# Spectra by array halves in layer 0, and other step weights, in a four-layer image network

## The chip, the cores and the metric

The kernel runs on one core of one Trainium2 chip. The metric is the device time of one execution in microseconds (us). Times of single instructions, waits and stages come from one profiled execution.

The engines that matter: TensorE (PE; its weight loads stand apart as PEld), VectorE (DVE), ScalarE (ACT), GpSimd (POOL), and SyncE (SP), which only issues transfers. Each works through its own instructions in order, and the engines wait for each other by semaphores. Matmuls write to PSUM, which is eight banks of 128 x 512 floats.

## The reference

The input is four images of 48 channels, 256 x 256, in float32. Four layers follow, each as `x = x + L(gn(x))`, where `gn` is a group norm over three channels and the whole image.

```python
# layer 0: 1x1 conv to 288 channels, 3x3 depthwise conv, then per 8x8 patch
q, k, v = split(dwconv(conv1x1(x)), 3)                 # 96 channels each
out = irfft2(rfft2(q_patch) * rfft2(k_patch))          # 8x8 patches
out = conv1x1(v * layernorm_over_channels(out))
# layer 1: 1x1 conv, filter in the patches' spectrum, 3x3 depthwise, gelu gate, 1x1 conv
# layer 2: box means, the box of each pixel from a small conv net:
out = (A + D - B - C) / area                           # 4 bilinear samples of the 2-d running sum
# layer 3: 1x1 conv, 3x3 depthwise, gelu gate, 1x1 conv, filter in the patches' spectrum
```

A patch's spectrum is computed as a product with a small matrix of cosines and sines. Of an 8 x 8 real patch it has 64 real numbers: 34 cosine sums ("every": four frequencies that are their own mirror, and 30 pairs) and 30 sine sums ("pairs").

## The kernel before

**Two streams.** `run` (L1210) lets two generators take turns. Stream "a" does layers 0 and 1 of image 0, then of images 1, 2 and 3, then layer 3 of all four. Stream "b" does the first statistics of the images and some weights, then layer 2 of images 0 to 3. Layer 2 of an image starts when its layer 1 is done, so it is issued beside layers 0 and 1 of the next image; layer 2 of image 3 stands beside layer 3 of images 0 to 2, and layer 3 of image 3 must wait for it. Each `yield` gives a weight; the stream with the smaller sum of weights goes next (`advance`, L1228), and a stream that must wait for the other takes over its sum. The weights thus settle how the two streams' instructions are mixed in every engine's order. A scheduler may still move instructions within that order, except the ones passed through `pinned`. Stream "a" issues its transfers on SP's queue, stream "b" on GpSimd's; each stream has its own PSUM banks, five for "a" and two (with a third for weights) for "b". A bank is handed out anew when its last reader is done.

**Layer 0** (L392) goes by units of four blocks of 128 pixels, 128 units an image, as a pipeline. In step n: `convolve` of unit n (24 full records and 8 tail records on TensorE into four banks, L353 and L361; four copies to `qkv` by ScalarE, L434); `inverse` of unit n-2; `spectra` of n-1; `turn` of n-5 (four transposes, L493, and a copy, L495); `project` of n-6 for every other strip (L505, L507); `gate` of n-4. A block has 128 pixels, that is two patches, one on partitions 0 to 63 and one on 64 to 127. `spectra` treats both at once: the 128 spectral numbers of the two patches are 68 cosine rows and 60 sine rows, so a matmul with 128 x 128 matrices gives q (L438), k (L439) and k with cosine and sine exchanged (L440), 384 columns each. ScalarE copies q (L442), VectorE makes the two products t1 and t2 (L445, L446), and `inverse` adds two matmuls (L454, L455) in one bank. VectorE takes the statistics of the result (L457), and ScalarE copies it to `o` (L458).

`convolve2` (L346) treats the ninth tap's rest, 58 rows, in `tails`: its two row halves of the array, partitions 0 to 57 and 64 to 121, hold two different pixel rows.

**Layer 1** (L585) has three stages: A, 1x1 conv, stored to DRAM (L623); B, filter and depthwise conv by channel group (L654, L667, L668); C, turn and project (L741, L754).

**Layer 2** (L838) first makes the running sums (`sums`, L774), then works through 32 pieces, two to a strip of eight rows (both image halves). A piece has four steps. In each, GpSimd issues 16 gathers into one of three buffers `V` (L974), and VectorE weights and adds the buffer of the step before (`add`, L981: L985, four times L987, L988). Convolution (L876, L885), projection (L901) and boxes for later pieces are mixed in. When both pieces of a strip are done, `finish` (L992) loads the strip of x, turns the result on TensorE (L999), adds it (L1006), and stores the strip. It is called in the three steps after the strip's last: the load stands in the first of these, the store in the last, both on GpSimd's queue between gathers.

**Layer 3** (L1066) is a pipeline of 128 units an image, two yields each.

Of the kernel before, what the change touches and what calls it, by code (L numbers as in the profile page):

```python
# [8 lines left out]
F32 = mybir.dt.float32  # L9
# [10 lines left out]
NS = 16  # L20
CP = 2 * C
PW = 258
# [36 lines left out]
def constants():  # L59
    own, pairs = _frequencies()  # L60
    every = own + pairs
# [5 lines left out]
    f1, f2, a1, a2 = (np.zeros((128, 128)) for _ in range(4))  # L67
    for k in range(2):
        px = slice(64 * k, 64 * k + 64)
        for i, f in enumerate(every):  # L70
            r, w = 34 * k + i, (1 if f in own else 2) / 64
            f1[px, r] = cos[f]
            a1[r, px] = w * cos[f]
            if f in pairs:
                f2[px, r] = -sin[f]
                a2[r, px] = -w * sin[f]
        for i, f in enumerate(pairs):
            r, w = 68 + 30 * k + i, 2 / 64
            f1[px, r] = -sin[f]
            f2[px, r] = cos[f]  # L80
            a1[r, px] = -w * cos[f]
            a2[r, px] = -w * sin[f]
# [69 lines left out]
    for a in range(2):  # L152
# [9 lines left out]
        "c_dft": np.stack([f1, f2, a1, a2, rf, rf.T], 1),  # L162
# [13 lines left out]
class Net:  # L176
    def __init__(self, ctx, tc, a, out):
# [13 lines left out]
        dft = self.load("c_dft", [128, 6, 128])  # L191
        self.f1, self.f2, self.a1, self.a2, self.rf, self.ri = (dft[:, i, :] for i in range(6))
# [199 lines left out]
    def layer0(self, x, mr, y):  # L392
        nc, a = self.nc, self.a
        st = self.stat.tile([CP, 129, 6], F32, name=self.nm("st"), tag="st" + self.stream, bufs=1)
        with ExitStack() as ctx:
# [40 lines left out]
            def spectra(t):  # L436
                q1, k1, k2 = self.bank(), self.bank(), self.bank()
                nc.tensor.matmul(v3(q1), self.f1, t.qkv[:, :, 0:96], start=True, stop=True)  # L438
# [3 lines left out]
                nc.scalar.copy(qs[:], q1[:, 0:384])  # L442
                t.t1 = sb.tile([128, 384], F32, name="t1", tag="t1")
                t.t2 = sb.tile([128, 384], F32, name="t2", tag="t2")
                nc.vector.tensor_mul(t.t1[:], qs[:], k1[:, 0:384])  # L445
                nc.vector.tensor_mul(t.t2[:], qs[:], k2[:, 0:384])  # L446

            def inverse(t):
# [5 lines left out]
                nc.tensor.matmul(po[:, 0:384], self.a1, t.t1[:], start=True, stop=False)  # L454
                nc.tensor.matmul(po[:, 0:384], self.a2, t.t2[:], start=False, stop=True)  # L455
# [382 lines left out]
    def layer2(self, x, mr, y, table):  # L838
# [3 lines left out]
        with ExitStack() as ctx:  # L842
# [148 lines left out]

            def finish(t, j):  # L992

                if j == 0:
                    t.xt = sb.tile([CP, 8, PW], F32, name="xt", tag="xt", bufs=1)
                    self.load_rows(t.xt, x, 8 * t.s, 8)
# [8 lines left out]
                v = t.xt[:, 2 * j : 2 * j + 2, 1:257]  # L1005
# [3 lines left out]
                if j == 3:  # L1009
                    self.store_rows(y, t.xt, 8 * t.s, 8)  # L1010
# [10 lines left out]
            for n in range(2):  # L1021
                for h in range(2):
                    convolve(pieces[n], h)
                    look(pieces[n + 1], h)
                    for j in range(2):
                        project(pieces[n], 2 * h + j)
                if n == 0:
                    boxes(pieces[0])
                yield 30
            last, done = None, None  # L1030
            for n in range(len(pieces) + 1):
                t = piece(n)
                for h in range(4):
# [10 lines left out]
                    yield 11  # L1044
# [17 lines left out]
                    yield 11  # L1062
# [3 lines left out]
    def layer3(self, x, mr, y):  # L1066
        nc, a = self.nc, self.a
        with ExitStack() as ctx:
# [97 lines left out]
            for n in range(len(units) + 7):  # L1166
# [5 lines left out]
                yield 4  # L1172
# [10 lines left out]
                yield 4  # L1183
# [120 lines left out]
```

## Time and profile before

| | us |
|---|---|
| runs, median of 3 | 20775.92 (20766.17 to 20789.14) |
| profiled execution | 20767.55 |
| its span on the core | 20765.8 |
| TensorE busy | 18830.0 (91%) |
| VectorE busy | 10830.0 (52%) |
| GpSimd busy | 8656.1 (42%) |
| ScalarE busy | 5784.0 (28%) |

By the first and last instructions of their lines, the stages of the profiled execution are: layer 0 of image 0 from 145 to 1967 us and its layer 1 from 1975 to 3536, both without gathers; then three times about 4165 us for layers 0 and 1 of images 1 to 3 beside layer 2 of the image before (layer 0 of image 1 from 3606 to 5651, its layer 1 from 5679 to 7699); then layer 3 of images 0 to 2 beside layer 2 of image 3, from about 16040 to 19733; then layer 3 of image 3 alone, to the end. Layer 1's stages took 352, 905 and 276 us in image 0 and 535, 1145 and 280 us in image 1. The gathers run from 3996 to 7395, 8155 to 11564, 12324 to 15723 and 16546 to 19709 us.

The page's 40 slices are 519 us each. A digit is the busy share in tenths; PEclk is the granted clock of TensorE in the same way. In the tables of groups a line gives instructions, busy time, mean length, and the idle time of the engine just before them with what ended it.

### The profile page before, as it was taken

To read this page: it belongs to the slowest core of one execution; us is meant where nothing else is said; L and a number is where in the kernel's file an instruction comes from. 1 tells how busy PE (TensorE), PEld (TensorE's weight loads), DVE (VectorE), ACT (ScalarE), POOL (GpSimd) and SP (SyncE) were. 2 spreads that over 40 slices of the span, in tenths; PEclk is the share of its full clock that TensorE was granted. 3 is DMA by queue.
4 is the path that set the end of the run, shared out by engine and by line. 5 is a ranking of instruction groups with operands and counts; after the bars stand their busy time and mean duration, and the time that the engine had idled before them with its cause. 6 is when DMAs were issued, how large, how long until landed. Compare 5 with 4: busy or idle time off the path is not lost.

```text
span 20769.8 us, 232624 instructions
## 1 busy us (share of the span) xinstructions
PE 18834.6 (91%) x79032; PEld 11959.3 (58%) x79032; DVE 10828.5 (52%) x21947; ACT 5789.6 (28%) x12185; POOL 8657.6 (42%) x8899
## 2 busy tenths in 40 slices
PE   7998798999878889998788899997888999999999
PEld 4566335666543346665433466654334787878888
DVE  4544322477764544777645437776554255555511
ACT  2333212333331123333311233333112211111111
POOL 1000000177754511777545216775552066666600
PEclk9899799999968999999689999996889999999999
DMA  4623876555588975555889755558898566767633
GB/s 113 134 57 80 232 215 201 133 129 131 128 244 223 239 214 133 129 132 126 239 229 233 222 131 126 130 127 232 232 234 225 142 150 150 158 149 158 147 76 74
DMA packets 2494455, 3403.86 MB, mean 164 GB/s; under 512 B 595078, under 2 KB 2069630, under 8 KB 2382731
## 3 DMA queue, kind: packets, MB, share of 16 engines
q1 hardware_dynamic: 1906184, 2081.72, 38.6%
q0 software_dynamic: 452944, 1110.52, 21.7%
q10 hardware_dynamic: 134144, 196.73, 4.2%
q8 instruction: 635, 10.40, 0.2%
q14 instruction: 548, 4.49, 0.1%
HBM read 2450.46 MB, written 802.77 MB: 157 GB/s over the span
## 4 chain that ended last, share of the span: by engine, by line
PE 73%; DMA 14%; DVE 5%; POOL 3%; issue 2%; SPq 1%; ACT 1%; ACTq 0%; DVEq 0%; POOLq 0%
PE ps L353 23%; PE ps L361 5%; PE ps L876 5%; PE ps L654 4%; PE ps L668 3%; PE ps L667 3%; DMA ct<-cD 3%; PE ps L623 3%; PE ps L754 3%; POOL V L974 3%; PE ps L1120 2%; PE ps L901 2%; PE ps L505 2%; PE ps L811 2%; PE ps L741 1%
## 5 line engine op out<-in xcount | busy, mean ns | idle before, releaser
L974 POOL DMA_INDIRECT V<-t,idx x8192 | 8242.8, 1006 | 4831.8 <-issue 2343.8
L353 PE MATMUL ps<-W,A 128*128 128x288 f32 (+1 forms) x24576 | 5571.9, 375 | 96.1 <-DMA A<-x 26.9
L353 PEld LDWEIGHTS ps<-W,A 128*128 128x128 f32 x24576 | 4298.4, 192 | 1246.5 <-issue 530.0
L214 POOL DMA_DIRECT2D X<-x x192 | 144.0, 755 | 4247.4 <-DMA x<-xt 3037.6
L987 DVE TENSOR_TENSOR V<-V 128x1536 f32<-128x1536 f32 (+3 forms) x2048 | 1843.6, 901 | 19.5
L985 DVE TENSOR_TENSOR V<-V,w 128x3072 f32<-128x3072 f32 x512 | 1713.4, 3346 | 28.4 <-DMA V<-t,idx 18.0
L654 PE MATMUL ps<-hg,ct 128*128 128x512 f32 x2304 | 1268.7, 678 | 404.0 <-DMA ct<-cD 322.8
L623 PE MATMUL ps<-win,xp 48*128 48x288 f32 x4096 | 1097.0, 626 | 512.0 <-DVE xp L610 231.2
L434 ACT COPY qkv<-ps 128x288 f32<-128x288 f32 x2048 | 764.4, 401 | 2680.0 <-PE ps L353 1197.9
L876 PE MATMUL ps<-A,W 128*96 128x512 f32 x3072 | 1490.3, 621 | 3.0 <-issue 3.0
L668 PE MATMUL ps<-yh,ht 65*128 65x512 f32 x2304 | 1187.1, 661 | 141.4 <-DMA yh<-ys 123.7
L361 PE MATMUL ps<-W,B 58*128 58x288 f32 (+1 forms) x8192 | 1267.9, 392 | 29.5 <-DMA B<-x 16.7
L1100 DVE TENSOR_TENSOR gp<-gl,ps 128x192 f32<-128x192 f32 x1024 | 354.3, 352 | 1710.2 <-ACT gl L1099 1709.4
L457 DVE BATCH_NORM_STATS2 bs<-ps 128x6 f32<-128x96 f32 x2048 | 389.7, 252 | 1638.1 <-PE ps L455 1637.9
L667 PE MATMUL ps<-ys,tt 128*128 128x512 f32 x2304 | 1177.7, 633 | 66.3 <-DVE ys L658 33.1
L623 PEld LDWEIGHTS ps<-win,xp 48*128 48x128 f32 x4096 | 692.9, 276 | 884.9 <-ACT hs L630 286.4
L654 PEld LDWEIGHTS ps<-hg,ct 128*128 128x128 f32 x2304 | 472.5, 212 | 1047.2 <-issue 940.4
L1099 ACT ACTIVATE gl<-ps 128x192 f32<-128x192 f32 x1024 | 332.1, 331 | 2614.0 <-PE ps L353 2359.1
L672 DVE TENSOR_TENSOR gt<-gl,ps 128x512 f32<-128x512 f32 x576 | 395.5, 688 | 1248.1 <-PE ps L668 1247.6
L361 PEld LDWEIGHTS ps<-W,B 58*128 58x128 f32 x8192 | 762.5, 187 | 450.8 <-issue 343.1
L876 PEld LDWEIGHTS ps<-A,W 128*96 128x96 f32 x3072 | 488.8, 169 | 859.0 <-issue 846.0
L658 DVE COPY ys<-ps 128x512 f32<-128x512 f32 x576 | 397.1, 690 | 1087.2 <-PE ps L654 885.7
(182 smaller groups left out, 24313.1 us busy)
## 6 DMA issues: line engine op xcount, KB each, us to landing
hD<-hs SPq DMA_DIRECT2D x64, 4608.0 KB
hg<-hD SPq DMA_DIRECT2D x288, 1024.0 KB
gD<-gt SPq DMA_DIRECT2D x144, 1024.0 KB
gs<-gD SPq DMA_DIRECT2D x64, 2304.0 KB
V<-t,idx POOLq DMA_INDIRECT x8192
A<-x SPq DMA_DIRECT2D x512, 193.5 KB
xt<-x SPq DMA_DIRECT2D x256, 387.0 KB
A<-x ACTq DMA_DIRECT2D x512, 193.5 KB
```

Of the source, the lines that this page charges most:

```text
L353: nc.tensor.matmul(to(q, b), A[:, r + q, 128 * b + g : 128 * b + g + 128], W[:, g, :], start=b == 0 and g == 0, stop=b == 1 and g == 2,)
L361: nc.tensor.matmul(to(q, b), B[p, r // 2, 128 * b : 128 * b + 128], W[p, 3, :], start=b == 1, stop=b == 0)
L434: nc.scalar.copy(t.qkv[:, 2 * q + b, :], banks[2 * b + q][:, 0:288])
L623: nc.tensor.matmul(ps[:, :288], xp[64 * h : 64 * h + 48, b, :], win[64 * h : 64 * h + 48], start=True, stop=True,)
L654: nc.tensor.matmul(ps[:].rearrange("p (s n) -> p s n", n=32), ct[:, c, :], hg[:, :, c, :], start=True, stop=True)
L667: nc.tensor.matmul(order(ps[:]), to[:, q, :], pick(yo, 128, q), start=True, stop=False)
L668: nc.tensor.matmul(order(ps[:]), ho[:, q, :], pick(yho, NZ, q), start=False, stop=True)
L754: nc.tensor.matmul(pp[:CP, :], pr[:, q, :], got[q][:], start=q == 0, stop=q == 2)
L876: m = nc.tensor.matmul(to[q], W[:, g, :], A[:, q:4:2, g : g + 256], start=q == 0 and g == 0, stop=q == 1 and g == 2,)
L974: nc.gpsimd.indirect_dma_start(out=V[:, k, 4 * cr : 4 * cr + 4, :].rearrange("p e c -> p (e c)"), out_offset=None, in_=table, in_offset=ba ...
L985: self.pinned(nc.vector.tensor_mul(Vm, Vm, wm.unsqueeze(2).to_broadcast([128, 64, 48])))
L987: nc.vector.tensor_add(V[:, :, 0:n, :], V[:, :, 0:n, :], V[:, :, n : 2 * n, :])
```

## The change

1. **Layer 0's spectra.** The matrices are now for one patch: 64 x 64 `f1` and `f2`, and `back` with `a1` above `a2`. `fq` holds `[f1 f1]` and `fk` holds `[f1 f2]` for each half of the partitions, so that one matmul with 64 rows gives 128 outputs for one patch. `spectra` makes four such matmuls instead of three full ones, q and k for each half, into four banks; ScalarE copies q twice, and VectorE makes two products, one for each half. `inverse` makes two matmuls with all 128 rows and 64 outputs, one into the lower and one into the upper half of the bank's partitions.
2. **Layer 2's strips.** `finish` neither loads nor stores. `fetch` loads a strip (the first before the loop), and the store and the next load are issued in the second and the fourth step of the piece after the one in which the strip is finished; the last store follows the loop. There is still one buffer.
3. **Step weights.** The two yields of a gather step go from 11 to 12, those of layer 3 from 4 to 4.4.

```diff
@@ layer0
             def spectra(t):
-                q1, k1, k2 = self.bank(), self.bank(), self.bank()
-                nc.tensor.matmul(v3(q1), self.f1, t.qkv[:, :, 0:96], start=True, stop=True)
-                nc.tensor.matmul(v3(k1), self.f1, t.qkv[:, :, 96:192], start=True, stop=True)
-                nc.tensor.matmul(v3(k2), self.f2, t.qkv[:, :, 96:192], start=True, stop=True)
-                qs = sb.tile([128, 384], F32, name="qs", tag="qs")
-                nc.scalar.copy(qs[:], q1[:, 0:384])
-                t.t1 = sb.tile([128, 384], F32, name="t1", tag="t1")
-                t.t2 = sb.tile([128, 384], F32, name="t2", tag="t2")
-                nc.vector.tensor_mul(t.t1[:], qs[:], k1[:, 0:384])
-                nc.vector.tensor_mul(t.t2[:], qs[:], k2[:, 0:384])
+                q, k = [self.bank() for _ in range(2)], [self.bank() for _ in range(2)]
+                half = lambda p: slice(64 * p, 64 * p + 64)
+                for to, f, c in ((q, self.fq, 0), (k, self.fk, 96)):
+                    for p in range(2):
+                        nc.tensor.matmul(
+                            v3(to[p]), f[half(p), :], t.qkv[half(p), :, c : c + 96], start=True, stop=True
+                        )
+                t.product = []
+                for p in range(2):
+                    qs = sb.tile([128, 384], F32, name="qs", tag=f"qs{p}")
+                    nc.scalar.copy(qs[:], q[p][:, 0:384])
+                    t.product.append(sb.tile([128, 384], F32, name="tp", tag=f"tp{p}"))
+                    nc.vector.tensor_mul(t.product[p][:], qs[:], k[p][:, 0:384])
...
                 po = self.bank()
-                nc.tensor.matmul(po[:, 0:384], self.a1, t.t1[:], start=True, stop=False)
-                nc.tensor.matmul(po[:, 0:384], self.a2, t.t2[:], start=False, stop=True)
+                for p in range(2):
+                    nc.tensor.matmul(
+                        po[64 * p : 64 * p + 64, 0:384], self.back, t.product[p][:], start=True, stop=True
+                    )
@@ layer2
+            strip = {}
+
+            def fetch(s):
+                if s < NS:
+                    strip[s] = sb.tile([CP, 8, PW], F32, name="xt", tag="xt", bufs=1)
+                    self.load_rows(strip[s], x, 8 * s, 8)
+
             def finish(t, j):
-                if j == 0:
-                    t.xt = sb.tile([CP, 8, PW], F32, name="xt", tag="xt", bufs=1)
-                    self.load_rows(t.xt, x, 8 * t.s, 8)
...
-                v = t.xt[:, 2 * j : 2 * j + 2, 1:257]
+                v = strip[t.s][:, 2 * j : 2 * j + 2, 1:257]
...
-                if j == 3:
-                    self.store_rows(y, t.xt, 8 * t.s, 8)
...
+            fetch(0)
             last, done = None, None
             for n in range(len(pieces) + 1):
...
-                    yield 11
+                    yield 12
...
+                    if n % 2 and n > 2 and h == 1:
+                        self.store_rows(y, strip[n // 2 - 1], 8 * (n // 2 - 1), 8)
+                    if n % 2 and n > 2 and h == 3:
+                        fetch(n // 2)
...
-                    yield 11
+                    yield 12
+            self.store_rows(y, strip[NS - 1], 8 * (NS - 1), 8)
@@ layer3
-                yield 4
+                yield 4.4
...
-                yield 4
+                yield 4.4
```

More of the change, by code (lines that the diff above doesn't have):

```diff
@@ L63, in constants @@
     sin = {f: _waves(f)[1].ravel() for f in every}
[L67 to L82, printed above, removed]
+    f1, f2, a1, a2 = np.zeros((64, 64)), np.zeros((64, 64)), np.zeros((64, 64)), np.zeros((64, 64))
+    for i, f in enumerate(every):
+        w = (1 if f in own else 2) / 64
+        f1[:, i] = cos[f]
+        a1[i] = w * cos[f]
+        if f in pairs:
+            f2[:, i] = -sin[f]
+            a2[i] = -w * sin[f]
+    for i, f in enumerate(pairs):
+        f1[:, 34 + i] = -sin[f]
+        f2[:, 34 + i] = cos[f]
+        a1[34 + i] = -2 / 64 * cos[f]
+        a2[34 + i] = -2 / 64 * sin[f]
+    first, second = np.tile(np.hstack([f1, f1]), (2, 1)), np.tile(np.hstack([f1, f2]), (2, 1))
+    back = np.vstack([a1, a2])
     rf, pick = np.zeros((128, 128)), np.zeros((40, 128))
@@ L161, in constants @@
         "c_ident": np.eye(128),
-        "c_dft": np.stack([f1, f2, a1, a2, rf, rf.T], 1),
+        "c_dft": np.hstack([first, second, rf, rf.T, back]),
         "c_pick": pick,
@@ L190, in __init__ @@
         self.ident = self.load("c_ident", [128, 128])
[L191 to L192 removed]
+        dft = self.load("c_dft", [128, 576])
+        self.fq, self.fk, self.rf, self.ri = (dft[:, 128 * i : 128 * i + 128] for i in range(4))
+        self.back = dft[:, 512:576]
         self.sel = self.load("c_sel2", [CP, 506])
```

## The prediction

> **What bounds the kernel now.** I read the page first, by engine and by slice:
>
> ```profile
> span 20765.8 us, 232624 instructions
> ...
> PE 18830.0 (91%) x79032; PEld 11956.8 (58%) x79032; DVE 10830.0 (52%) x21947; ACT 5784.0 (28%) x12185; POOL 8656.1 (42%) x8899
> ...
> PE   7998798999878889998788899987888999999999
> ...
> POOL 1000000177754511777545117775552066666600
> PEclk9899799999968999999689999996888999999999
> ...
> PE 72%; DMA 14%; DVE 6%; POOL 4%; issue 2%; SPq 1%; ACT 1%; ACTq 0%; DVEq 0%; POOLq 0%
> ```
>
> TensorE is busy for 91% of the span and makes 72% of the chain that ended last, so removed TensorE time is removed time, except where that engine waits. Where it waits is seen in the stretches (columns: length, then busy time of TensorE, its weight load, VectorE, ScalarE, GpSimd, then granted clock, DMA share, GB/s):
>
> ```profile
> 4672.00:5191.00 519.00, 511.97 (x2073) 319.52 (x2072) 384.70 (x856) 200.81 (x447) 370.83 (x363) 1.00 0.54 132
> ...
> 6230.00:6749.00 519.00, 443.57 (x1024) 188.47 (x1025) 258.16 (x382) 82.50 (x136) 248.65 (x262) 0.87 0.88 228
> ...
> 19720.00:19760.00 40.00, 14.29 (x66) 10.46 (x66) 22.72 (x51) 0.26 (x1) 1.10 (x2) 0.63 0.36 82
> ```
>
> Layer 0 beside layer 2's gathers (first row) is TensorE alone: 512 of 519 us. Layer 1 beside gathers (second) is held by DMA: 88% of the DMA engines, 228 GB/s. At the last seam (third), where layer 3 of image 3 waits for layer 2 of image 3, TensorE works 14 us in 40.
>
> One unit of layer 0, alone on TensorE, from the timeline (start, length, engine, line; "x" counts records, two for each of these matmuls):
>
> ```profile
> 1500.47 3.08 PE L353 MATMUL ps<-W,A 128*128 128x288 f32 x12
> ...
> 1503.47 1.24 PE L361 MATMUL ps<-W,B 58*128 58x288 f32 x8
> ...
> 1504.64 3.18 PE L353 MATMUL ps<-W,A 128*128 128x288 f32 x12
> ...
> 1507.66 0.81 PE L454 MATMUL ps<-t,c_dft_sb 128*128 128x384 f32 x2
> ...
> 1508.30 0.81 PE L455 MATMUL ps<-t,c_dft_sb 128*128 128x384 f32 x2
> ...
> 1508.95 0.81 PE L438 MATMUL ps<-qkv,c_dft_sb 128*128 128x384 f32 x2
> ...
> 1509.15 0.76 DVE L457 BATCH_NORM_STATS2 bs<-ps 128x6 f32<-128x96 f32 x4 [5.55 <-PE ps L455]
> ...
> 1509.80 0.48 ACT L442 COPY qs<-ps 128x384 f32<-128x384 f32 x1 [1.54 <-PE ps L438]
> 1510.17 0.49 ACT L458 COPY o<-ps 128x384 f32<-128x384 f32 x1
> ...
> 1510.88 0.60 PE L493 MATMUL ps<-c_ident_sb,un 128*96 128x128 f32 x4
> ```
>
> From L454's start to L493's is 3.22 us for ten records, so 0.322 us a record of 384 columns; 0.242 for 288 in proportion.
>
> **Layer 0, passes.** Before, ten records in a row: 3.22 us. After, the four forward matmuls use 64 rows of the array each, as two pairs (4 places of 0.322 if a pair runs together), and the two inverse ones 64 columns each, as one pair (2 places). That is 1.93 us: 1.29 us less, for 512 units 660 us. That row halves run together the trace shows at L361: eight records, also two row halves, take 1.17 us from their start to the next L353, not 8 x 0.242 = 1.94. No column pair is in this trace. Its bounds are together (2 places) and one after the other (4 places, 0.645 us a unit or 330 us more). I take together, the row pairs being nearest.
>
> **Layer 0, changes of mode.** The same rows price the switch. From 1500.47 to 1507.66 is 7.19 us; 24 full records and 4 pair places are 28 x 0.242 = 6.78; the rest, 0.41, pays for going into row halves and out, 0.2 each. The same reckoning on layer 2's L876 and L885 (512 columns) gives 0.17; I take 0.19. The Trainium skill speaks against the change here ("TensorEngine Tiling (Array Packing)", Key Properties): changing the mode drains the array. In the instruction order of the two programs the changes of mode go from 3038 to 4702: full to columns, to rows, to full again, and one more where layer 2's work falls between. 1664 x 0.19 = 316 us. By passes alone the gain would be 660; with the drain it is 344. The skill's other rule ("TensorE: Matmul & The Clock Gate", Measured speedup vs the span model) has three column tiles at 2.38 times, not 3; at that yield the column pair's 0.645 becomes 0.81, 86 us over the kernel. No run here shows which; that goes into the range.
>
> **Layer 0, banks.** Stream "a" has five PSUM banks. Spectra takes four instead of three, and the five are then all in recent use when the turn and the next convolve (or project) start. In the changed program's bank assignment the turn mostly takes q's first bank, freed by the first copy of q; the next matmul takes the inverse's bank, freed by the copy of o, which stands on ScalarE behind the first copy of q and waits for L457. In an undisturbed unit, counted from the end of the convolve: inverse ends 0.93, q pair 1.77, first copy 2.29, turn could start at 2.34 and does (release takes 0.05); o is copied by 2.78, the next matmul could start at 2.78 to 2.88 and its bank is free at 2.83. Just in time, so no cost. But if VectorE is late with L457, TensorE now stops at once; before, that bank had over a microsecond more. Worked out from the trace's records of L455 and L457: where no work of layer 2 lies between inverse and turn (318 of the 512 units in the changed order), L457 ends on average 1.20 us after L455, usually 0.80. 0.4 x 318 = 127 us at most; some of it was paid before, so I take 100. In 36 such units the turn takes the inverse's bank: 0.5 x 36 = 19. The other 194 have 0.4 to 4 us of layer 2 between. Queued behind the stopped turn is all of TensorE, of both streams. The second copy of q (512 x 0.48 = 246 us) is ScalarE time, hidden by an engine that is 28% busy; it follows the copy of o and feeds a product that the convolve's third or fourth bank waits for, some 1 us later. VectorE's two products keep number and size. Layer 0 in all: 344 - 100 - 19 = 225 us off.
>
> **Layer 2's strips.** On GpSimd's queue the store waited for the last add and the gathers stood behind it:
>
> ```profile
> L214 POOL DMA_DIRECT2D x<-xt x128 | 70.0, 552 | 386.2 <-DVE xt L1006 348.3 <-DVE V L987 36.0 <-DMA V<-t,idx 1.6
> ...
> 4803.39 0.98 POOL L974 DMA_INDIRECT V<-t,idx  x1 [0.30 <-issue]
> ...
> 4804.68 0.95 POOL L974 DMA_INDIRECT V<-t,idx  x1 [0.30 <-issue]
> ```
>
> 348 us of waits go, since the store moves two steps later. The number of transfers stays; each is past two to three steps of gathers, on GpSimd alone, SP's queue is not passed. The new load waits for the store issued two steps (some 45 us) earlier: free. Gathers follow each other every 1.25 to 1.29 us, so a step of 16 needs 20 us, while a step beside layer 0 lasts 24 (from one strip's L999 to the next, eight steps, some 190 us). TensorE covers the wait, so 0; at the ends -15 (L974 as V is 3% of the chain) and 0.
>
> **Step weights, the seam between layers 1 and 2.** A step is a `yield`, and its weight says how much of the other stream is issued meanwhile. Layers 0 and 1 of an image weigh 135 x 14 + 1612 = 3502. Layer 2 weighed 328 + 60 + 132 x 22 = 3292, and so ended 210 early; with 24 it weighs 3556 and ends 54 late. So 5 gather steps leave layer 1's first two stages (9.7 and 6.0 us a step there, by the first image's lengths without gathers: 352 and 905 us against 535 and 1145), some 3.5 leave layer 0 (6.7), and 8 go to layer 1's last stage, where GpSimd idled but TensorE is 93% busy and DMA moves 225 GB/s (7420 to 7690 us). 35 + 23 us saved against 8 steps of 1.57 MB at 240 GB/s, 52: about 7 us an image, 20 in all; -80 to +60 as bounds, as that stage has room or has none.
>
> **Step weights, the end.** The lateness adds up to 162, and layer 3's 3 x 135 x 8.8 = 3564 against 3556 + 162 leaves 154, or 6.4 steps of gathers, with no layer 3 beside them; before 52, or 2.4. VectorE's order says the same: after the last gate of layer 3's third image stand six weightings of V, two before. V has three buffers, so three of the six are gathered by then and three remain: 3 x 20 us, less the few us by which the last weighting follows sooner. 55 us on the path, with TensorE idle (bounds 20 and 85).
>
> **Sum.** -225 + 0 - 20 + 55 = -190 us. The profiled execution took 20767.6 (span 20765.8 and 1.8 around it), which gives 20577.6; the median of the runs shown is 8.4 above it, so 20586, rounded 20590.
>
> **Rivals.** (1) Columns one after the other. For: no row here shows them overlapping, and both read all 128 rows. Against: row halves do overlap. +330: about 20920, slower. It decides from 58% of the pair's place lost on (190 of 330). (2) The bank waits and the last seam eat it: VectorE's long weightings (L985, 3.35 us each) hold L457 in most units, layer 1's last stage has no DMA left. Layer 0 keeps 100, balance +40, end +70: about 20780, no change. (3) The waits fall where layer 2's matmuls fill them and layer 1 gains from the even spread: 344 + 80 - 20: about 20370. (4) No halves run together at all: 12 places instead of 6, 990 more than in my sum, about 21580; the L361 rows speak against it.
>
> **Chances.** Likeliest case 0.58 (20480 to 20690); rival 1 0.14; rival 2 0.16; rival 3 0.10; rival 4 0.02. About 0.2% (41 us) is what can be told from no change. Faster: 0.58 + 0.10 = 0.68; within: 0.10, the greater part of rival 2; slower: its rest, 0.06, and rivals 1 and 4, 0.22. Leaving out the outer halves of rivals 1 and 3 and rival 4 gives 20420 to 20920.
>
> **What would show it.** Right: the two inverse matmuls start within some ns of each other, 0.645 us a pair with about 0.2 after each change of mode; layer 0 beside layer 2 shorter by some 60 us an image; gathers up to the end of each layer 1; a gap of some 100 us at the last seam with GpSimd at 20 us a step. Wrong: inverse records 0.32 us apart all four; idle time before the turn and the next convolve, put down to the copies of q and o, above 0.4 us a unit; a seam of 150 us or more.

## The result and the profile after

The changed kernel takes 20747.47 us, median of 12 runs (20734.86 to 20772.32), against 20778.06 for the kernel before, measured beside it (12 runs, 20753.48 to 20832.62). The ratio is 0.9984, 95% interval 0.9975 to 0.9992: 31 us less, where 190 were forecast. That is within the 0.2% which the prediction counts as no change, though the interval leaves out 1. The profiled execution took 20743.78 us, its span 20741.6.

The page of the kernel after, the lines that answer to those shown of before:

```profile
span 20741.6 us, 235448 instructions
...
PE 18569.8 (90%) x80056; PEld 11448.5 (55%) x80056; DVE 10811.4 (52%) x21947; ACT 5932.4 (29%) x12663; POOL 8613.0 (42%) x8899
...
PE   7998798999878889998788899987888999999999
...
POOL 1000000266654441666444416664445056666600
...
PE 5%; DVE 0%; DMA 0%; ACT 0%; issue 0%; SPq 0%; POOL 0%; DVEq 0%
```

TensorE's busy time fell by 260 us (18830.0 to 18569.8), where the passes less the changes of mode were to take off 344; its mean granted clock fell from 0.918 to 0.909. The span fell by 24. So 236 us of work were turned into idle time. GpSimd's row shows the gathers spread over more of layer 1 (the 4 and 5 where there was a low digit). The chain of waits reaches back over only the last 5% here, so it can't be set beside the 72% of before.

The stretches of the kernel after, of the same length as those of before and 80 and 75 us earlier, and the last seam (columns: length; busy time of TensorE, weight load, VectorE, ScalarE, GpSimd; granted clock, DMA share, GB/s):

```profile
4592.00:5111.00 519.00, 492.33 (x2154) 287.82 (x2154) 366.92 (x820) 211.62 (x480) 344.14 (x338) 0.99 0.51 125
6155.00:6674.00 519.00, 465.69 (x1073) 195.26 (x1072) 260.58 (x392) 87.72 (x145) 249.59 (x267) 0.90 0.92 232
...
19655.00:19755.00 100.00, 17.74 (x65) 12.61 (x66) 53.74 (x77) 0.26 (x1) 59.36 (x60) 0.53 0.45 110
```

Beside gathers, layer 0 leaves TensorE idle for 27 us in 519, where 7 were idle before. In the last seam TensorE works 18 us in 100.

The unit of layer 0 alone on TensorE, from the timeline after:

```profile
1501.41 0.87 PE L460 MATMUL ps<-tp,c_dft_sb 128*64 128x384 f32 x4
1502.21 1.56 PE L443 MATMUL ps<-qkv,c_dft_sb 64*128 64x384 f32 x8
...
1503.16 0.48 ACT L449 COPY qs<-ps 128x384 f32<-128x384 f32 x1 [1.24 <-PE ps L443]
1503.53 0.48 ACT L465 COPY o<-ps 128x384 f32<-128x384 f32 x1
...
1503.70 0.64 PE L500 MATMUL ps<-c_ident_sb,un 128*96 128x128 f32 x4
...
1503.90 0.50 ACT L449 COPY qs<-ps 128x384 f32<-128x384 f32 x1
...
1504.18 3.08 PE L354 MATMUL ps<-W,A 128*128 128x288 f32 x12
...
1511.46 0.87 PE L460 MATMUL ps<-tp,c_dft_sb 128*64 128x384 f32 x4
```

From L460's start to L460's next start a unit lasts 10.05 us, 0.80 less than the 10.85 between two such starts of L454 before (the first of these, at 1507.66, stands in the prediction):

```profile
1518.51 0.81 PE L454 MATMUL ps<-t,c_dft_sb 128*128 128x384 f32 x2
```

The first two records of the column pair start 6 ns apart (1501.415 and 1501.421), so the pair runs together. The turn L500 starts 0.06 us after q's first copy, and the next convolve 0.17 us after the copy of `o`: just in time, as the prediction had it.

By stage, from the ends of the projections of layers 0 and 1 (L505 and L754 before) and the ends of layer 3's images, in us:

| stage | before | after | spectra only | weights only | spectra, statistics from the copy |
|---|---|---|---|---|---|
| layer 0, image 0 | 1966.8 | 1886.4 | 1904.0 | 1964.6 | 1884.0 |
| layer 0, images 1, 2, 3 | 2114.7, 2113.0, 2109.7 | 2087.7, 2096.3, 2064.8 | 2109.3, 2113.0, 2113.5 | 2090.9, 2096.7, 2081.3 | 2086.5, 2096.9, 2085.7 |
| layer 1, images 1, 2, 3 | 2047.9, 2053.9, 2051.4 | 2055.1, 2073.2, 2101.7 | 2052.1, 2053.3, 2048.8 | 2057.0, 2080.1, 2096.3 | 2046.8, 2054.7, 2053.7 |
| layer 3, images 1, 2, 3 | 1175.0, 1164.2, 1024.9 | 1195.6, 1173.0, 1059.7 | 1181.7, 1163.9, 1024.3 | 1193.0, 1171.1, 1060.4 | 1178.6, 1168.4, 1015.0 |

Layer 0 of image 0 gained 80 us. Layer 0 of images 1 to 3, beside gathers, gained 89 in all; layer 1 of these lost 77, and layer 3 of them 64. The column with the spectra alone says more: there layer 0 of images 1 to 3 gains nothing.

One of the 22 runs with the strips alone, below, took 48802.22 us at a granted clock of 0.365, against 0.917 to 0.920 in the other 21; it is left out of the ratio, and why it was slow isn't known.

### The profile page after: what moved, and what is told of

Read it like the earlier page. It is cut to its first block, busy times and chain, and to the rows that moved or that the text cites. A ratio compares the mean times of both kernels' runs of the same rounds, so it can differ in the third digit from the quotient of the medians.

```text
span 20763.8 us, 235448 instructions
## 1 busy us (share of the span) xinstructions
PE 18568.4 (89%) x80056; PEld 11454.7 (55%) x80056; DVE 10812.9 (52%) x21947; ACT 5934.1 (29%) x12663; POOL 8600.7 (41%) x8899
## 5 line engine op out<-in xcount | busy, mean ns | idle before, releaser
L354 PEld LDWEIGHTS ps<-W,A 128*128 128x128 f32 x24576 | 4351.3, 194 | 1354.1 <-issue 572.6
L362 PE MATMUL ps<-W,B 58*128 58x288 f32 (+1 forms) x8192 | 1221.5, 392 | 26.0 <-DVE tp L451 12.0
L637 ACT COPY hs<-ps 128x288 f32<-128x288 f32 x1024 | 634.0, 654 | 1075.7 <-PE ps L630 815.3
```

Of the source, the lines that this page charges most:

```text
L354: nc.tensor.matmul(to(q, b), A[:, r + q, 128 * b + g : 128 * b + g + 128], W[:, g, :], start=b == 0 and g == 0, stop=b == 1 and g == 2,)
L362: nc.tensor.matmul(to(q, b), B[p, r // 2, 128 * b : 128 * b + 128], W[p, 3, :], start=b == 1, stop=b == 0)
L637: nc.scalar.copy(hs[:, :, h, b], ps[:, :288])
```

## The experiments

In the first four runs "W" is the theory that the step weights give the gain back, "S" that the copies of q and `o` come late because VectorE holds them (narrow: by the statistics, which the copy of `o` waits for; wide: by all that stands ahead of these on VectorE), "P" that layer 2's pace on GpSimd sets layer 0's length beside gathers. All ratios are against the kernel before on the same chip; the third column is (ratio - 1) x 20780 us, and the text compares these. Each has an interval of 15 to 31 us either way, so a difference of two is good to some 30 to 45 us.

| run | median, us | us by ratio | ratio, 95% interval |
|---|---|---|---|
| after | 20747.47 | -33 | 0.9984, 0.9975 to 0.9992 |
| spectra only | 20662.99 | -96 | 0.9954, 0.9941 to 0.9967 |
| strips only | 20780.14 | +19 | 1.0009, 1.0001 to 1.0016 |
| weights only | 20843.39 | +91 | 1.0044, 1.0031 to 1.0057 |
| after, weights undone | 20679.98 | -81 | 0.9961, 0.9948 to 0.9974 |
| after, layer 3's weight 4.65 | 20712.04 | -98 | 0.9953, 0.9939 to 0.9967 |
| spectra, statistics from the copy | 20638.17 | -160 | 0.9923, 0.9910 to 0.9937 |
| before, statistics from the copy | 20746.14 | -21 | 0.9990, 0.9981 to 0.9998 |
| before, no additions | 20621.85 | -172 | 0.9917, 0.9902 to 0.9931 |
| spectra, no additions | 20466.01 | -328 | 0.9842, 0.9827 to 0.9857 |
| spectra, statistics, no additions | 20378.22 | -376 | 0.9819, 0.9807 to 0.9832 |
| before, half the gathers | 20313.75 | -453 | 0.9782, 0.9769 to 0.9794 |
| spectra, half the gathers | 20168.40 | -609 | 0.9707, 0.9694 to 0.9720 |

### The three parts alone

**The spectra alone**: the diff of layer 0 as shown above, nothing else.

> Only the spectra by halves; strips and step weights as before. Theory W (the step weights gave the gain back: some 54 us at the last seam and some 25 us an image in layer 1): layer 0 keeps its gain in all four images, 170 to 220 us off, about 20580. Theory S (the gain is lost in images 1 to 3 to waits inside layer 0, TensorE waiting for the copies of q and o that VectorE holds up beside the gathers): only image 0's 80 us and some 15 us for each other image remain, 110 to 130 us off, about 20650. Theory P (layer 2 and not TensorE sets the pace of images 1 to 3): about 80 us off, 20695.

**The strips alone**: `fetch` and the moved store, nothing else.

> Only layer 2's strips stored and loaded steps apart; spectra and step weights as before. Theories W and S: no effect, within 20 us of 20776, since TensorE covers GpSimd's wait. Theory P: GpSimd's 348 us of waits were part of the pace, so 30 to 100 us off.

**The step weights alone**:

```diff
-                    yield 11
+                    yield 12
...
-                yield 4
+                yield 4.4
```

> Only the step weights 12 and 4.4; spectra and strips as before. Theory W: slower by 100 to 140 us (54 at the last seam, the rest in layer 1), about 20890. Theory S: slower by the last seam alone, 40 to 60 us, about 20830. Theory P: the seam and a longer layer 2 in each image, slower by 100 us and more.

**All of the change but the weights** (the yields back to 11 and 4):

> The changed kernel with the step weights put back to 11 and 4. Theory W: faster than the changed kernel by 100 to 140 us, about 20620. Theory S: faster by the last seam alone, 40 to 60 us, about 20695. Theory P: as S or less.

The spectra are worth 96 us, where 225 were forecast. The strips are worth nothing or a little less. The weights cost 91 alone and 48 in company (-81 to -33), where 35 were forecast (-20 and +55).

**Where the spectra's gain goes.** The groups of TensorE's instructions in layer 0 of image 1 before (3606 to 5651 us; columns: busy, mean ns, idle just before them and what ended it):

```profile
L353 PE MATMUL ps<-W,A 128*128 128x288 f32 x3025 | 807.8, 416 | 16.4 <-DVE xt L507 7.7 <-ACT qs L442 7.4 <-ACT o L458 1.1
...
L505 PE MATMUL ps<-u,pr 96*96 96x512 f32 x256 | 120.5, 592 | 0.8 <-ACT u L495 0.8
...
L493 PE MATMUL ps<-c_ident_sb,un 128*96 128x128 f32 x512 | 77.6, 274 | 17.3 <-DVE un L487 17.3
```

The same groups with the spectra alone (3537 to 5576 us):

```profile
L354 PE MATMUL ps<-W,A 128*128 128x288 f32 x3024 | 820.3, 421 | 25.7 <-ACT qs L449 24.6 <-ACT o L465 0.8 <-DVE tp L451 0.3
...
L512 PE MATMUL ps<-u,pr 96*96 96x512 f32 x255 | 130.7, 636 | 30.4 <-ACT qs L449 21.4 <-ACT o L465 8.2 <-ACT u L502 0.8
...
L500 PE MATMUL ps<-c_ident_sb,un 128*96 128x128 f32 x512 | 83.8, 287 | 30.7 <-DVE un L494 17.8 <-ACT o L465 12.7 <-ACT qs L449 0.3
```

The waits for `qs` and `o` go from 8.5 us to 68.0: convolve, project and turn now take banks that are freed by these copies. Over images 1 to 3 they come to 135 us for `qs` and 62 for `o`, in 61 and 32 stops (those between 0.3 and 6.5 us), against 18 and 3 before: 176 us more. And the granted clock in these three stages goes from 0.98, 0.98 and 0.99 to 0.97 in each. TensorE's busy time fell by 66, 58 and 61 us instead of the 86 that passes and changes of mode should give, some 24 short an image. So 86, less 24, less 59 of waits leaves next to nothing an image, which is what the stages show.

The trace says where these 24 went. The clock is granted whole or by half, and the halves come in stretches of 3.4 us or multiples of that: 68 stretches with 433 us in these three stages, against 27 with 256 us before. Half of the 178 us more is 89 us lost, 30 an image, enough for the 24. For 40 of the 68 stretches the longest stop of TensorE in the 7 us before is one for `qs` or `o`, for 5 of the 27 before. So the stops cost twice: once as idle time, and again as slow matmuls behind them. In the stretches around one such stop, which lasts from 5313.8 to 5316.3 (columns as above, the clock third from the end):

```profile
5300.00:5313.20 13.20, 13.20 (x50) 5.82 (x49) 6.86 (x21) 4.92 (x9) 11.04 (x8) 1.00 0.52 122
5313.20:5316.00 2.80, 0.62 (x6) 0.37 (x4) 0.00 (x0) 0.22 (x1) 2.11 (x3) 0.99 0.99 230
5316.00:5322.70 6.70, 6.39 (x10) 3.28 (x11) 4.10 (x8) 2.55 (x7) 5.01 (x5) 0.50 0.56 133
5322.70:5340.00 17.30, 17.30 (x90) 11.98 (x89) 10.48 (x18) 5.84 (x15) 13.58 (x13) 1.00 0.42 116
```

### Who holds the copies

**Statistics from the copy**, with the spectra:

```diff
-                for b in range(4):
-                    nc.vector.bn_stats(t.strip.bs[:, 4 * t.j + b, :], po[:, 96 * b : 96 * b + 96])
                 nc.scalar.copy(
                     t.strip.o[:, 4 * t.j : 4 * t.j + 4, :].rearrange("p a b -> p (a b)"), po[:, 0:384]
                 )
+                for b in range(4):
+                    nc.vector.bn_stats(t.strip.bs[:, 4 * t.j + b, :], t.strip.o[:, 4 * t.j + b, :])
```

> The spectra by halves alone, with the statistics taken from the copy of o in SBUF, beside the kernel before on a chip where that takes about 20770. Theory S, narrow: 60 to 180 us off the spectra alone (0.9954 of the kernel before), 0.987 to 0.9925. Theory S, wide (the two products take the place), and theory P: 0.994 to 0.997; S wide with new waits of TensorE for the products, P without.

The same groups of this run, layer 0 of image 1 (3520 to 5537 us):

```profile
L354 PE MATMUL ps<-W,A 128*128 128x288 f32 x3038 | 821.4, 420 | 24.9 <-ACT qs L449 20.7 <-DVE tp L451 4.2
...
L512 PE MATMUL ps<-u,pr 96*96 96x512 f32 x256 | 129.9, 631 | 17.9 <-ACT qs L449 17.1 <-ACT u L502 0.8
...
L500 PE MATMUL ps<-c_ident_sb,un 128*96 128x128 f32 x512 | 83.3, 286 | 17.4 <-DVE un L494 17.4
```

The waits for `o` are gone. Over images 1 to 3 that is 62 us; the waits for `qs` fall too, from 135 to 109, and those for other tiles (VectorE's products above all) grow by some 40. The run is 64 us under the spectra alone. It is the fastest kernel here that computes everything: 20638 us, below both. Its control is the kernel before with the same edit:

> The kernel before with one change: the statistics of each projected strip are read from the strip's copy in on-chip memory instead of from the product's own place, so that the copy need not wait for them. It is the control of the run that did the same on top of the spectra by halves (there 64 us less than with the spectra alone). If the late copies are a cost that the spectra by halves brought (S, narrow), the whole rows of the array have slack for them and this run is within 25 us of the kernel before. If the statistics cost the same in both (VectorE held, whatever TensorE does), it gains 50 to 80 us as well, and then the spectra by halves are worth no more than the 100 us they gave alone.

It gains 21 us, so some two thirds of the 64 are a cost that the spectra by halves brought. The ratios alone, each from another chip, would not settle this; the stages do. Layer 0 of images 1 to 3 is 67 us shorter with the edit on top of the spectra (6336 to 6269 us in all) and 6 longer with it in the kernel before (6337 to 6344). The late `o` stops TensorE only since banks come round at once.

**VectorE's additions out.** The next two leave out the sum over the sixteen weighted corners of each box, before and with the spectra (`for n in (8, 4, 2, 1)` becomes `for n in ()`), to shorten what stands ahead of the statistics on VectorE:

> The kernel before without the four additions of V in a gather step; the sum over corners is left out, so 3.6 us of VectorE's work a step is gone. Theory S: TensorE waited little for VectorE, so 0 to 80 us off. Theory P: the gathers' step is GpSimd's own and does not change, 0 to 30 us off.

> The spectra by halves alone, also without these four additions. Theory S (either form): with VectorE freer its holds of TensorE shrink, and the halves earn in images 1 to 3 too: 180 to 300 us less than the kernel before without the additions. Theory P: the distance stays what it is with the additions, about 100 us.

The spectra are worth 156 us between these two, 60 more than with the additions in, though less than the 180 to 300 that S expected; layer 0 of images 1 to 3 gains 80 here (6278 to 6198 us in all). The kernel before gained 172 us without the additions, more than either theory allowed it; 59 of these are in layer 0 of images 1 to 3, and where the rest comes from was not followed. In layer 0 of image 1 the wait for `o` is 3.4 us now; that for `qs` is still 48.7. The third leaves the same sum out and reads the statistics from the copy:

> Spectra by halves, statistics from the copy, and no additions of the sixteen weighted corners (left out: the sum over corners). Beside the kernel before without the additions (166 us under the kernel before). If VectorE's hold on the copies is all that takes the gain of images 1 to 3 (S), both of its holds are shorter now and the spectra and statistics together are worth 220 to 340 us against that kernel: about 20300 to 20400. If the pace of the gathers on GpSimd sets these images (P), it stays at the 150 us that the same edit gave with the additions in: about 20470.

With it the spectra and the statistics are worth 204 us against the kernel before without additions, a little under the 220 to 340 that S expected. The `o` waits are zero, the `qs` waits 36 us an image: 105 in all.

**GpSimd freed.** To test P, two of the four corner rows of each box are neither gathered nor weighted nor added (left out: the lower half of the box corners):

```diff
-                    for cr in range(4):
+                    for cr in range(2):
...
-                for n in (8, 4, 2, 1):
+                for n in (4, 2, 1):
```

> The kernel before with two of the four corner rows gathered, weighted and added for each box (left out: the lower half of the sixteen box corners). It takes half of the GpSimd issue and half of VectorE's box work out of every step. As the base of the next run: S and P both expect it under the kernel before without additions, 150 to 300 us under the kernel before, because VectorE holds the copies for less and the gathers end 10 us of 23.6 earlier in each step.

> The spectra by halves, on top of the same two corner rows of four. If the pace of the gathers on GpSimd held images 1 to 3 (P), which the runs without additions could not free, the full price of the passes and mode changes now shows, 250 to 340 us against the half-gather kernel before. If VectorE's hold on the copies of the projected strips does it (S), the difference stays at 130 to 200 us, as without the additions, because the weighting and the statistics still stand ahead of the copies.

GpSimd's busy time in layer 0 of image 1 is halved (1162.65 us before, 597.85 and 600.79 in these two). The first of the two gains 453 us, more than the 150 to 300 expected; layer 1, which isn't the subject here, is over 100 us shorter in each of images 1 to 3. The spectra are worth 156 us between them, the same as without additions. VectorE's load in this stage is the same in the two pairs (1119.05 and 1118.51 us without additions, 1124.28 and 1123.14 here), so what differs is GpSimd, and it makes no difference: P falls. Layer 0 of image 1 in the second of the two, the same groups:

```profile
L354 PE MATMUL ps<-W,A 128*128 128x288 f32 x3036 | 818.3, 419 | 28.6 <-ACT qs L449 25.5 <-DVE tp L451 2.6 <-ACT o L465 0.5
...
L512 PE MATMUL ps<-u,pr 96*96 96x512 f32 x255 | 132.2, 643 | 23.1 <-ACT qs L449 21.7 <-ACT u L502 1.1 <-ACT o L465 0.3
...
L500 PE MATMUL ps<-c_ident_sb,un 128*96 128x128 f32 x512 | 83.5, 286 | 19.2 <-DVE un L494 14.1 <-ACT o L465 4.8 <-ACT qs L449 0.3
```

The waits for `o` have fallen as without the additions; the waits for `qs` are where they were, 47.5 us. Neither VectorE's additions nor the gathers hold these. One part VectorE's statistics hold, as the 26 us above show; the rest is seen in one of the stops, from the timeline of the run with the spectra alone:

```profile
5311.69 1.56 PE L443 MATMUL ps<-qkv,c_dft_sb 64*128 64x384 f32 x8
5311.80 0.68 ACT L895 ACTIVATE hm<-ps,b 96x512 f32<-96x512 f32 x1 [2.07 <-PE ps L883]
5311.80 1.27 ACTq L281 DMA_DIRECT2D A<-x  x3
...
5313.11 0.91 ACTq L287 DMA_DIRECT2D B<-x  x2
5313.18 0.64 PE L500 MATMUL ps<-c_ident_sb,un 128*96 128x128 f32 x4
...
5314.06 0.37 ACTq L284 DMA_DIRECT2D B<-c_inside  x1
5314.47 1.27 ACTq L287 DMA_DIRECT2D B<-x  x3
...
5315.78 0.86 ACT L449 COPY qs<-ps 128x384 f32<-128x384 f32 x2 [3.30 <-DMA A<-x]
...
5316.31 1.17 PE L512 MATMUL ps<-u,pr 96*96 96x512 f32 x1 [2.49 <-ACT qs L449]
```

The products for q and k are done at about 5313.2, the first copy begins at 5315.78. In between ScalarE runs nothing: it issues loads of rows for layer 2's next convolve, eleven for each half step at 0.3 to 0.46 us each, nine of them in a row here behind layer 2's activation. They stand on its queue ahead of layer 0's copies and are not counted as busy. Theory D: this is the other holder. In layer 0 of images 1 to 3 the `qs` stops of this run last 135 us; for 71 of them ScalarE was issuing, for 58 it was executing something: 37 of these are the copy of q itself, which ends the stop, and 16 the square root in layer 0's own statistics (L479, with its table load), which is gone from the stops when the statistics come from the copy. In the run with spectra and statistics and without the additions it is 72 of 105. The kernel before issues the same 440 loads an image (173 us), but its `qs` waits are 18 us in three images; there a bank more lies between.

**The loads on SP's queue.** The last three runs issue these loads from SP, in the kernel before, with the spectra, and with spectra and statistics:

```diff
-                    t.G[h] = self.columns2(x, 128 * t.i + 8 * t.s + 4 * h, 4, cols, nc.scalar.dma_start)
+                    t.G[h] = self.columns2(x, 128 * t.i + 8 * t.s + 4 * h, 4, cols, nc.sync.dma_start)
```

> The kernel before with one change: the eleven loads of rows for each half step of layer 2's convolve are issued on SP's queue instead of ScalarE's. Control for the next run. In layer 0 of image 1 the kernel before waits only 8.8 us for the copies qs and o, so D (ScalarE's issues stand ahead of layer 0's copies) expects at most 25 us from this in layer 0 of images 1 to 3. What SP's queue does with them in layer 1 is open, -40 to +60 us; it is the same in the next run.

> The spectra by halves with the same move of issues. In the run with the spectra alone TensorE waits for the copies qs 46 us in layer 0 of image 1, and in the eight longest of the nine of these stops that were followed back, ScalarE does not run before the copy: it issues eleven loads after layer 2's gates, 3.3 us at a stretch. If that is the cause (D), these waits fall below 15 us, layer 0 of images 1 to 3 shortens by 30 to 45 us each, and the spectra are worth 190 to 240 us against the control. If VectorE holds the copies (S), the waits stay above 35 us and the worth is about 100 us.

> Spectra by halves, statistics from the copy, and the loads on SP's queue: both holds of the copies taken away with the whole computation in place. D and S together: waits for qs and o below 10 us in layer 0 of image 1, and 230 to 290 us under the control; if only VectorE's hold counted, no better than the statistics alone gave (150 us under the kernel before).

These, and the three below, fell on two other chips on which the kernel before takes 25779 and 25510 us: each stage that holds gathers is some 400 to 670 us longer there, so their times say little about the chips of the other runs. The ratios were 1.0099 (1.0078 to 1.0120), 1.0130 (1.0105 to 1.0155) and 1.0118 (1.0096 to 1.0140): all slower than before, and the second is slower than the first. So SP's queue is no place for these loads; layer 3 of images 1 and 2 grew most, from 1773 and 1696 us (before with statistics, on the other of these chips) to 1920 and 1827. The `qs` stops of layer 0 of images 1 to 3, counted between 0.3 and 6.5 us as above, are 14.5 us with spectra, statistics and the loads on SP, and 44.4 with spectra and statistics alone. That fits D, but across two chips and among longer stops it doesn't show it: with these in, the sums are 37 and 102, and in the control, the kernel before with the loads on SP, they are 219. D rests on the timeline and the overlap, and the experiment that should have shown it is inconclusive.

Three of the edits above also ran on the second of these chips, where the kernel before takes 25510 us:

> The spectra by halves alone, and besides VectorE takes the statistics from the copy of o in SBUF, so that ScalarE's copy of o, the second copy of q behind it and the inverse's bank no longer wait for VectorE. Theory S in its narrow form (the copies of q and o, held up by the statistics, take the gain in images 1 to 3): their waits, 67 us an image, go, and the time falls by 60 to 180 us against the spectra alone, to 20480 to 20600. Theory S in its wide form (whatever VectorE still owes, the two products first, takes the place): within 30 us of the spectra alone, the waits standing at the products. Theory P (layer 2 sets the pace): as the wide form, but with the gathers' step unchanged and no new waits on TensorE.

> The kernel before with the statistics taken from the copy of o in SBUF. Theories S and P: within 30 us of the kernel before, since there TensorE hardly waits for these copies (some 9 us an image).

> The changed kernel with layer 3's step weight at 4.65 instead of 4.4: layer 2 of image 3 then ends 49 before layer 3's third image instead of 154 after it. Theory W: the last seam's 35 to 60 us come back, 20685 to 20715, with layers 0 and 1 as in the changed kernel. If the weights cost in layers 0 and 1 alone: no change, 20747.

They gave 0.9951 (0.9938 to 0.9965), 0.9965 (0.9951 to 0.9979) and 0.9921 (0.9907 to 0.9935). There the kernel before gained 89 us by the statistics, where its expectation allowed 30, and the spectra on top of them were worth 36 us more; the other chips repeat neither (21 and 139). Their layers with gathers hold waits of up to 32 us that no engine of the core ends (last section), so the text goes by the runs of the table.

### The last seam

The kernel after at the last seam, from the timeline (in brackets the idle time before, and what ended it):

```profile
19676.15 1.09 PE L1012 MATMUL ps<-c_ident_sb,res 128*96 128x128 f32 x4 [0.52 <-DVE res L995]
19693.68 1.09 PE L1012 MATMUL ps<-c_ident_sb,res 128*96 128x128 f32 x4 [16.45 <-DVE res L995]
19738.91 1.09 PE L1012 MATMUL ps<-c_ident_sb,res 128*96 128x128 f32 x4 [44.14 <-DVE xt L1019]
```

Layer 2's last turns wait 16 and 44 us with no layer 3 left to run; before, no wait of this kind is over 1 us. From the stop at the last strip of layer 3's third image on, TensorE's waits of over 1 us add up to 88 us (9.36, 2.69, 16.45, 44.14, 6.19, 1.08, 7.73) and to 30 before (8.10, 6.60, 8.02, 7.65): 57 more. The test takes the lateness away with a larger weight for layer 3, so that layer 2 gets ahead:

```diff
-                yield 4.4
+                yield 4.65
```

> The changed kernel with layer 3's step weight at 4.65, beside the kernel before on such a chip. Theory W: the seam's 35 to 60 us come back against the changed kernel (0.9984), 0.9955 to 0.997, the stretch from the end of layer 1 of image 3 to the end shorter and layers 0 and 1 unchanged. Otherwise 0.998 to 0.999.

The timeline of this run at the same place:

```profile
19664.22 0.60 PE L1012 MATMUL ps<-c_ident_sb,res 128*96 128x128 f32 x4
...
19705.07 2.81 PE L342 MATMUL ps<-wh,mt 128*74 128x192 f32 x8 [17.98 <-DVE mt L340]
19715.38 5.14 PE L354 MATMUL ps<-W,A 128*128 128x192 f32 x15 [7.50 <-DMA A<-x]
```

No turn waits any more, and what is left of the seam is layer 3's own start. Layer 3 of images 1 to 3 is 14 us longer than before in all, where it was 64, and the run is 65 us under the kernel after by the ratios, 45 by the medians beside their own base. So most of what the weights cost is the last seam.

## Why the prediction was wrong, step by step

**Passes: right.** 0.80 us a unit are saved where layer 0 stands alone. The column pair runs together, 0.80 us from its first record to the next matmul's against 0.645 and one change of mode, so rivals 1 and 4 fall.

**Changes of mode: right in size.** A unit that stands alone has three changes more, and 1.29 - 3 x 0.19 is 0.72 where 0.80 were measured, so a change cost 0.16. 344 us in all is 86 an image; image 0 gained 80, in the run with the statistics 83, with the spectra alone 63. That these are near 86 is in part chance: 128 such units would be 103, and in image 0, too, the clock stood at half for longer (256, 256 and 287 us in these three runs, 242 before). The yield that the Trainium skill ("TensorE: Matmul & The Clock Gate", Measured speedup vs the span model) has for column tiles would have left 65; the trace shows no such loss for a pair.

**Banks: the step that failed.** It had "Layer 0, banks" at 100 + 19 us over all 512 units. Measured: 176 us more waiting in images 1 to 3 alone. VectorE's lateness with L457, the only cost that was reckoned, was priced too high: that part (`o`) came to 59 us more, and the statistics from the copy took 26 off the `qs` waits besides. What was missed is larger. The copies of q were held to be hidden "by an engine that is 28% busy". A busy share doesn't contain what the engine issues: on ScalarE's queue stand layer 2's activations and eleven loads for each half step, and the `qs` part came to 117 us more. That TensorE waits for these copies is measured; that the loads hold them is seen in the timeline and the overlap, not shown by taking them away. The prediction named 0.4 us a unit of such waits as a sign of being wrong; it is 198 us in 384 units, 0.52. A mean busy share is no cover for a copy that must start within 0.05 us. Beyond that the granted clock fell by 1 to 2 points in these stages, some 24 to 30 us an image, which no term held. 225 forecast, 96 measured.

**The sum of these reads back.** Of the 344 of passes and drain, the run with the spectra alone lost 176 to waits and 89 to the clock in images 1 to 3, and 22 to the clock in image 0. That leaves 57, and layer 0 of its profiled execution gained 64. The 96 are by the ratio of the medians; the profiled execution, at 20700.33 us, was 37 above the median of its six runs. With the `o` waits cut, each pair with its own control gives more: 139 (statistics from the copy), 156 (no additions), 156 (half the gathers).

**Strips: right at nothing, for a wrong reason.** The wait on GpSimd's queue did not go. The row of the store, after:

```profile
L215 POOL DMA_DIRECT2D x<-xt x128 | 70.2, 553 | 457.3 <-DVE xt L1019 425.4 <-DVE res L995 16.3 <-DVE V L994 7.4
```

It was 348 us before and is 338 with the strips alone. In the kernel before it consists of four waits of 110, 104, 105 and 30 us, each at the last strip of an image, when its gathers are over and nothing is queued behind. The row's sum was read as a wait at every strip.

**Step weights, between layers 1 and 2: wrong by some 30 us.** Forecast -20. In the run with the weights alone layer 0 of images 1 to 3 gained 68 us and layer 1 of them lost 80, so +12. The lateness does add up: layer 1 loses 9, 26 and 45. The 68 are the 23 an image that were forecast for layer 0. Layer 1's stages of images 1 to 3, by the first and last instructions of their lines on TensorE, in us:

| stage | before | after | weights only |
|---|---|---|---|
| A | 525, 529, 527 | 519, 532, 529 | 519, 533, 525 |
| B | 1163, 1164, 1161 | 1161, 1168, 1182 | 1165, 1164, 1182 |
| C | 280, 282, 284 | 294, 302, 312 | 296, 311, 308 |

(The 1145 us given for B of image 1 ahead of the prediction is 1163 by this count.) So two prices were wrong. The 35 us an image that were to come from A and B did not come, and in image 3 B is 21 longer; why isn't shown. C, priced at +52, cost 14 to 29: in image 1 of the kernel after TensorE is busy there for 280 us of 294, against 261 of 280 before, while the traffic rises from 218 to 268 GB/s, so layer 2's matmuls that moved into C lengthen it and not DMA.

**The end: right.** +55 forecast; the waits of the seam grew by 57, and the two turns alone hold 60.

**Rival 2 happened.** It had layer 0 at 100, which was 96, and 20780 us, no change. It was given 0.16, because the waits before were few. Its balance between layers 1 and 2 was +40 and came to +12, its end +70 and came to 57. But it blamed VectorE alone.

What stays open: whether the 70 us of issuing can be won by another order on ScalarE's queue, and whether the clock comes back when the stops go. A sixth bank for stream "a", the direct test of this step, was not run. Spectra by halves with the statistics from the copy and the larger weight for layer 3 together were not run.

## What to carry to other kernels

When an edit takes one more bank of a small pool, list for each bank who frees it, on which engine's queue, and what else stands on that queue there: activations and DMA issues of the other stream count, the engine's busy share doesn't. A gain seen in the stage where the engine works alone must be priced anew for each stage in which another stream shares its queues. And a mean wait of a group is placed in time before it is spent.

## What was not expected of the hardware

On two of the chips the same kernel took 23 to 24% longer, in the stages with gathers only: layer 0 of image 0, without gathers, is 1974.6 us there against 1971.8 for the same kernel elsewhere, and layer 0 of image 1 is 2772.8 against 2109.9. From the timeline of the kernel before with statistics from the copy, on such a chip, and its list of waits in layer 0 of image 1 (us in total, times, longest):

```profile
4731.08 0.38 DVE L907 TENSOR_TENSOR sc<-ps,b 128x208 f32<-128x208 f32 x1 [9.45 <-remote]
4731.12 1.31 ACT L434 COPY qkv<-ps 128x288 f32<-128x288 f32 x4 [15.98 <-remote]
...
4731.57 1.65 PE L438 MATMUL ps<-qkv,c_dft_sb 128*128 128x384 f32 x2 [4.73 <-ACT qkv L434]
...
ACT qkv L434 <- remote: 482.3, 49, 32.2
```

VectorE and ScalarE start again within 0.04 us of each other after waits that no engine of the core ends, TensorE behind them, while GpSimd goes on issuing gathers. What makes the chips differ isn't known.
